# The place of a transpose, of a residual read and of an unpacking step in a fused linear-attention and FP4 MLP kernel

## Chip, core and metric

The kernel runs on one NeuronCore of a Trainium2 chip. Its time is the device time of one execution, in microseconds. Three executions of the kernel before took 1330.86 to 1332.29 us, with a median of 1332.18. In the text, TensorE is PE (its weight loads are PEld), VectorE is DVE, ScalarE is ACT, GpSimd is POOL and SyncE, which issues nearly all transfers, is SP.

## What is computed

The input x has 4 batches of 512 tokens of width 512, all float32. Two pre-norm layers follow each other:

```
x = x + attn(layernorm(x))        # gated linear attention, 4 heads of 128, chunks of 128 tokens
x = x + ffn(layernorm(x))         # GEGLU with FP4 weights, 512 -> 4096 -> 512

attn, per batch, head and chunk:
  q, k, v = x@Wq+bq, x@Wk+bk, x@Wv+bv;  k = k / |k|
  alpha = sigmoid(x@Walpha+balpha);  beta = softplus(x@Wbeta+bbeta)
  cla = cumsum(log(alpha))          # inside the chunk
  y   = (q k^T * beta * exp(cla - cla^T), causal) v  +  exp(cla) * (q state)
  state = state * exp(cla_end) + v^T (k * beta * exp(cla_end - cla))

ffn:  W = lut[4-bit code] * scale  (one scale per 32 values)
  inter = gelu(x Wg^T) * (x Wu^T);  out = inter Wd^T
```

## The kernel before

Attention comes first, with 16 chunks (4 batches of 4). The outer loop steps over batches b and, inside, over twelve products j: four of v, four of q, four of k, one for each 128 tokens or head. Behind each product stands a call behind(p) with a running step number p, which adds the attention work of one chunk in three steps:

- p % 3 == 0: chunk_lead transposes k to kT (PE, then a copy on ACT), chunk_values makes kw and vb on POOL, chunk_decay makes the decay matrix dm (four exponentials on ACT, a causal select on POOL), qc and the scaled state. Then turn("f") runs.
- p % 3 == 1: turn("a") for the first norm, then chunk_scores: the scores sp on PE and dm = sp * dm on DVE (L589).
- p % 3 == 2: chunk_sums: dp (the state's increment) and yp (the chunk's output) on PE, the residual sum (L616) and its write to HBM, the statistics of the second norm (L310, L312), the new state (L620 or L622); settle() then makes the normalised tile hn (L320, after two small POOL operations).

turn("f") takes the hn that the last chunk_sums left. It transposes it by four matmuls into one PSUM bank, tp_f (L341), splits the result into three float32r pieces g0, g1, g2 (ACT L362, DVE L363 and L364), and issues three writes of 256 KB to HBM, h (L366). hn keeps its buffer until then.

The MLP takes a float32 product as products of such pieces. It is cut into 35 rounds, i = 0 to 34. Round i works on batch i % 4 and on up to four MLP tiles of 128 columns. For each tile gate_up makes two products, gate and up: twelve 128x512 matmuls each into the banks pa and pb (L696), from twelve tiles x that hold the round's transposed tokens, read back from h. pb goes through ACT (L701) and the sum through DVE (L702) into t. Gate ends with a gelu (L706), up with the multiplication by gate (L711), the split into three inter tiles i (ACT L714, DVE L716 and L717), and a call unpack(slots, upto). After each of the two products gate_up yields, and behind(p) is called, so that the last batch's chunks run between the first MLP products. At the end of a round, down makes the second product in eight PSUM banks p_d (L731), two for each 128 tokens, adds them to the residual a4 (L744, L745) and writes it. Tiles of the round but the last are summed first. The residual is four reads of 256 KB from HBM, asked for when the round begins.

Rounds 0 and 1 have one and two tiles, because the window of tiles slides in; in round 30, which the code makes short, and in round 33 there are two as well. These are the rounds with fewer than three tiles. Round 0 has no down of its own.

unpack(slots, upto) first issues the rounding of a weight tile that is waiting (ACT L194), and then takes up to slots pieces from a queue that turns 4-bit codes into float32r weights (DVE L179, L184, L188, L197, L200), where a piece is due by the MLP tile number upto.

The order on every engine is the order of these calls. Two resources couple the engines. SBUF tiles of 2 KB and 4 KB per partition come from lists of 42 and 24 buffers, handed out in the order in which they were given back: whoever gets a buffer waits for its last reader, which can be a transfer. PSUM has eight banks, also handed out in the order in which they were freed.

Of the kernel before, what the change touches and what calls it, by code (L numbers as in the profile page):

```python
# [35 lines left out]
def f32(t):  # L36
    return t.bitcast(F32)
# [3 lines left out]
def tile_gated_linear_attention__then__nvfp4_geglu(  # L41
# [27 lines left out]
    MC = 4  # L69
# [13 lines left out]
    def pool(where, name, bufs, **kw):  # L83
        return where.enter_context(tc.tile_pool(name=name, bufs=bufs, reuse_waits="tile", **kw))
# [6 lines left out]
    slots = pool(ctx, "slots", 1)  # L91
# [31 lines left out]
    def psum(name):  # L123
        return fps.tile([P, T], F32, tag="p", name=name)
# [133 lines left out]
    def more():  # L258

        if not loaded or len(two_k.free) < 3:  # L260
            return
        nxt, start = loaded.pop(0)
        fields, masked, scaled, hi, lo, mi = start()

        def third():
            scaled()
            rounding.append(hi)

        def fourth():
            while rounding:  # L270
                rounding.pop(0)()
            lo()
            fetch()

        queue.insert(max(len(queue) - 2, 0), (0, fields))
        queue.extend([(0, masked), (nxt, third), (nxt, fourth), (nxt, mi)])

    def unpack(slots, upto):
        while rounding:
            rounding.pop(0)()  # L280
        for _ in range(slots):
# [17 lines left out]
    def tile_of(t):  # L299
        return xf[t * P : (t + 1) * P, :]  # L300
# [34 lines left out]
    def turn(which):  # L335
        for done in [t for t in turned if t[1][0] in which]:
            turned.remove(done)
            hn, key, use = done
            tp = psum(f"tp_{key}")
            for k in range(KC):  # L340
                nc.tensor.transpose(tp[:, k * P : (k + 1) * P], f32(hn)[:, k * P : (k + 1) * P], ident)  # L341
            one_k.put(hn)
            use(tp)
# [106 lines left out]
    def gates_exp(b):  # L450

        za, az, ea, u = (gate(b, nm) for nm in ("za", "az", "ea", "u"))
        zb = zs[b][:, :, H:]
        nc.vector.tensor_scalar(th(za), zs[b][:, :, :H], -80.0, None, ALU.max)
        nc.vector.scalar_tensor_tensor(th(az), zb, -1.0, zb, ALU.mult, ALU.max)
        return lambda: (
            nc.scalar.activation(ea, za, AF.Exp, scale=-1.0),
            nc.scalar.activation(u, az, AF.Exp, scale=-1.0),
        )
# [116 lines left out]
    def chunk_scores(b, n):  # L576
        toks = slice(n * P, (n + 1) * P)
        sp = psum(f"sp_{b}_{n}")
        kT = ch.pop("kT")
        for h in range(H):  # L580
            nc.tensor.matmul(  # L581
                sp[:, h * P : (h + 1) * P], f32(kT)[:, h * P : (h + 1) * P],
                f32(q_sb[b][h // 2])[:, h % 2, toks], start=True, stop=True,
            )
        one_k.put(kT)
        if n == NCH - 1:
            two_k.put(*q_sb[b])
        dm = ch["dm"]
        nc.vector.tensor_tensor(f32(dm), sp, f32(dm), ALU.mult)  # L589
# [42 lines left out]
    def behind(p):  # L632
        b, j = divmod(p, 3 * NCH)
        cb, n = divmod((p - 2 * NCH - 1) // 3, NCH)
        chunk = 0 <= cb < B
        first = b < B
        if p % 3 == 0:
            exps = gates_exp(b) if first and j == 3 else None
            if chunk:
                chunk_lead(cb, n)  # L640
                chunk_values(cb, n)
            if first and j == 6:
                exps = gates_sums(b)
            if chunk:
                chunk_decay(cb, n)
            turn("f")
            if exps:
                exps()
        elif p % 3 == 1:
            turn("a")  # L650
            if chunk:
                chunk_scores(cb, n)
            if first and j == 7:
                gates_end(b)
            for t in early.get(p + 4, ()):
                if t[0] > 1:
                    xs[t] = load(tile_of(t[0] * NCH + t[1]), f"x{t[0]}_{t[1]}")
            t = (p - 2 * NCH - 2) // 3 + 1
            if 0 <= t < NT:
                acc[divmod(t, NCH)] = load(tile_of(t), f"xr{t}")  # L660
        else:
            if first and j == 5:
                gates_ln(b)
            if chunk:
                chunk_sums(cb, n)
            for t in early.get(p, ()):
                first_norm(*t, xs.pop(t))
            settle()
# [11 lines left out]
    x3 = [[] for _ in rounds]  # L680

    def load_x(i, which):
        if i < len(rounds):
            for j, k in which:
                x3[i].append(load(h2d[i % B][j][k], f"x_{i}_{j}_{k}"))

    def gate_up(mt, x, slots, upto, last, key):
        w3 = wgu[mt]

        def product(i):  # L690
            pa, pb = psum(f"pa_{i}_{key}"), psum(f"pb_{i}_{key}")
            for o, js in ((pa, (0, 1)), (pb, (2,))):
                for j in js:
                    for k in range(KC):
                        c = 2 * i + k // 2
                        nc.tensor.matmul(  # L696
                            o, w3[j][:, k % 2, c * P : (c + 1) * P], x[j * KC + k],
                            start=(j == js[0] and k == 0), stop=(j == js[-1] and k == KC - 1),
                        )
            t = one_k.get(f"t{i}_{key}")  # L700
            nc.scalar.activation(f32(t), pb, AF.Copy, scale=-1.0 / ONE_E)  # L701
            nc.vector.tensor_tensor(f32(t), pa, f32(t), ALU.add)  # L702
            return t

        g = product(0)
        nc.scalar.activation(f32(g), f32(g), AF.Gelu_apprx_tanh, scale=ONE_E)  # L706
        unpack(slots, upto)
        yield
        u = product(1)
        last()  # L710
        nc.vector.scalar_tensor_tensor(f32(u), f32(g), ONE_E, f32(u), ALU.mult, ALU.mult)  # L711
        one_k.put(g)
        ih, il, im = (one_k.get(f"i{j}_{key}") for j in range(3))
        nc.scalar.activation(ih, f32(u), AF.Copy, scale=HI)  # L714
        unpack(slots, upto)
        nc.vector.tensor_tensor(il, f32(u), f32(ih), ALU.subtract)  # L716
        nc.vector.scalar_tensor_tensor(im, f32(ih), ONE_E, f32(u), ALU.mult, ALU.subtract)  # L717
        one_k.put(u)
        yield
        return ih, il, im  # L720

# [29 lines left out]
    def residual(i):  # L751
        return [
            load(accd[t], f"acc_{i}_{t}") for t in range(i % B * NCH, (i % B + 1) * NCH)
        ]

    def mlp():
        for i, r in enumerate(rounds):
            ts = range(i % B * NCH, (i % B + 1) * NCH)
            ms = tiles[i]
            inter = []  # L760
            a4 = residual(i) if i > 0 else None
            ahead = [0] if i >= B - 1 else [i] if i > 0 else []
            for q, mt in enumerate(ms):
                if q in ahead:
                    load_x(i + 1, jk[:6])

                def last():

                    if q == len(ms) - 1:
                        one_k.put(*x3[i])  # L770
                        load_x(i + 1, jk[len(x3[i + 1]) :] if i + 1 < len(rounds) else [])

                inter.append((yield from gate_up(mt, x3[i], 2 if i == 1 else 1, r + MC, last, f"{i}_{mt}")))
                if mt == r and mt < tiles[-1][0]:
                    two_k.put(*wgu[mt])
            final = i + B >= len(rounds)
            dst = [of[t * P : (t + 1) * P, :] if final else accd[t] for t in ts]
            if i == 0:
                over = ms, inter
                continue  # L780
            if i == B:
                ms, inter = over[0] + ms, over[1] + inter
            down(ms, inter, a4, dst, f"{i}", i == len(rounds) - 1)
            if r >= 0 and r % 2 == 1 and r < tiles[-1][0]:
                two_k.put(*wd[r // 2])
            yield
# [138 lines left out]
```

## Time and profile before

| | |
|---|---|
| runs (us) | 1332.29, 1332.18, 1330.86; median 1332.18 |
| profiled execution | 1330.86 us, its span 1329.1 us |
| granted TensorE clock, mean | 0.997 |
| chain that ended last | PE 89%, DVE 4%, POOL 2%, ACT 2%, issue 2%, DMA 1% |
| PE by line in that chain | pa L696 34%, p_d L731 25%, pb L696 17% |
| matmul L696, L731, 128x512 | 390 and 391 ns each, starts 0.227 us apart |
| DMA | 236.57 MB, mean 178 GB/s |

Busy time is the time in which an engine ran an instruction; matmuls overlap, so two of 390 ns can start 0.227 us apart. Attention with the start runs to about 240 us, the last batch's chunks lie between MLP products until about 305 us, and from then on the MLP rounds follow each other: each of them takes 32.6 us, with TensorE at work without a pause, as in the windows between 320 and 1200 us.

### The profile page before, as it was taken

To read this page: it belongs to the slowest core of one execution; us is meant where nothing else is said; L and a number is where in the kernel's file an instruction comes from. 1 tells how busy PE (TensorE), PEld (TensorE's weight loads), DVE (VectorE), ACT (ScalarE), POOL (GpSimd) and SP (SyncE) were. 2 spreads that over 40 slices of the span, in tenths; PEclk is the share of its full clock that TensorE was granted. 3 is DMA by queue.
4 is the path that set the end of the run, shared out by engine and by line. 5 is a ranking of instruction groups with operands and counts; after the bars stand their busy time and mean duration, and the time that the engine had idled before them with its cause. 6 is when DMAs were issued, how large, how long until landed. Compare 5 with 4: busy or idle time off the path is not lost.

```text
span 1329.1 us, 16898 instructions
## 1 busy us (share of the span) xinstructions
PE 1299.9 (98%) x5800; PEld 1041.1 (78%) x5800; DVE 974.8 (73%) x1533; ACT 441.8 (33%) x777; POOL 123.9 (9%) x220
## 2 busy tenths in 40 slices
PE   7999999889999999999999999999999999999998
PEld 5576666677888888888888888888888888887886
DVE  3477766677767777777777778787877777877556
ACT  1333323443333333333333333333333333332332
POOL 1446453520000000000000000000000000000000
PEclk9999999999999999999999999999999999999999
DMA  7034435667645565655565656465555555555463
GB/s 238 9 96 120 126 104 193 227 218 251 195 152 196 177 199 182 200 172 194 176 207 172 200 172 205 157 210 180 193 172 193 180 184 184 180 175 197 152 248 132
DMA packets 173798, 236.57 MB, mean 178 GB/s; under 512 B 15760, under 2 KB 74128, under 8 KB 173712
## 3 DMA queue, kind: packets, MB, share of 16 engines
q1 hardware_dynamic: 173008, 235.20, 54.2%
q8 instruction: 46, 0.75, 0.2%
q10 hardware_dynamic: 704, 0.28, 0.1%
q14 instruction: 40, 0.33, 0.1%
HBM read 183.00 MB, written 52.43 MB: 177 GB/s over the span
## 4 chain that ended last, share of the span: by engine, by line
PE 89%; DVE 4%; POOL 2%; ACT 2%; issue 2%; DMA 1%; POOLq 0%; ACTq 0%; DVEq 0%
PE pa L696 34%; PE p_d L731 25%; PE pb L696 17%; PE pq L406 4%; PE pva L381 2%; PE pvb L388 2%; PE pk L418 1%; PE sp L581 1%; PE tp_a L341 0%; ACT sq L426 0%; POOL ss L431 0%; PE yp L611 0%; PE yp L609 0%; PE tp_f L341 0%; DVE t L702 0%
## 5 line engine op out<-in xcount | busy, mean ns | idle before, releaser
L696 PE MATMUL pa<-x,wgu 128*128 128x512 f32 x2048 | 506.9, 390 | 0.1
L696 PEld LDWEIGHTS pa<-x,wgu 128*128 128x128 f32 x2048 | 383.7, 188 | 79.6 <-DVE acc L745 0.3
L731 PE MATMUL p_d<-wd,i 128*128 128x512 f32 x1536 | 358.4, 391 | 3.5 <-DVE i L716 2.5
L731 PEld LDWEIGHTS p_d<-wd,i 128*128 128x128 f32 x1536 | 289.5, 189 | 66.6 <-DVE i L716 3.5
L696 PE MATMUL pb<-x,wgu 128*128 128x512 f32 x1024 | 273.7, 389 | 0.0
L701 ACT ACTIVATE t<-pb 128x512 f32<-128x512 f32 x256 | 151.4, 591 | 355.1 <-PE pb L696 348.8
L702 DVE TENSOR_TENSOR t<-pa,t 128x512 f32<-128x512 f32 x256 | 176.6, 690 | 95.6 <-ACT t L701 90.2
L696 PEld LDWEIGHTS pb<-x,wgu 128*128 128x128 f32 x1024 | 192.2, 188 | 40.0
L744 DVE SCALAR_TENSOR_TENSOR acc<-p_d,acc 128x512 f32<-128x512 f32 x136 | 93.3, 686 | 111.0 <-PE p_d L731 111.0
L714 ACT ACTIVATE i<-t 128x512 fp32r<-128x512 f32 x128 | 81.0, 633 | 196.2 <-DVE t L711 194.7
L706 ACT ACTIVATE t<-t 128x512 f32<-128x512 f32 x128 | 81.1, 634 | 153.2 <-DVE t L702 153.2
L716 DVE TENSOR_TENSOR i<-t,i 128x512 fp32r<-128x512 f32 x128 | 88.2, 689 | 24.1 <-ACT i L714 22.5
L745 DVE TENSOR_TENSOR acc<-acc,p_d 128x512 f32<-128x512 f32 x136 | 93.6, 688 | 15.0 <-PE p_d L731 0.7
L711 DVE SCALAR_TENSOR_TENSOR t<-t,t 128x512 f32<-128x512 f32 x128 | 88.7, 693 | 4.4
L717 DVE SCALAR_TENSOR_TENSOR i<-i,t 128x512 fp32r<-128x512 f32 x128 | 87.7, 685 | 0.0
L418 PE MATMUL pk<-wk,hT 128*128 128x512 f32 x128 | 57.4, 592 | 0.0
L406 PE MATMUL pq<-hT,wq 128*128 128x512 f32 x128 | 57.2, 592 | 0.0
L406 PEld LDWEIGHTS pq<-hT,wq 128*128 128x128 f32 x128 | 23.3, 190 | 24.0 <-issue 23.9
L418 PEld LDWEIGHTS pk<-wk,hT 128*128 128x128 f32 x128 | 23.2, 190 | 23.5 <-issue 23.4
L197 DVE SCALAR_TENSOR_TENSOR wgu<-wgu,w_gu 128x1024 fp32r<-128x1024 f32 x32 | 38.9, 1217 | 1.7 <-ACT wgu L194 1.6
L188 DVE SCALAR_TENSOR_TENSOR w_gu<-i_gu,sc_gu 128x1024 f32<-128x1024 f16 x32 | 39.8, 1243 | 0.0
L200 DVE TENSOR_TENSOR wgu<-wgu,wgu 128x1024 fp32r<-128x1024 f32 x32 | 39.0, 1218 | 0.0
(121 smaller groups left out, 893.3 us busy)
## 6 DMA issues: line engine op xcount, KB each, us to landing
x<-h SPq DMA_DIRECT2D x420, 256.0 KB
acc<-acc SPq DMA_DIRECT2D x256, 256.0 KB
h<-g SPq DMA_DIRECT2D x48, 256.0 KB
x<-in_x SPq DMA_DIRECT2D x16, 256.0 KB
pk_gu<-in_gate_p SPq DMA_DIRECT2D x32, 128.0 KB
sc_gu<-in_gate_s SPq DMA_DIRECT2D x64, 64.0 KB
pk_gu<-in_up_p SPq DMA_DIRECT2D x32, 128.0 KB
sc_gu<-in_up_s SPq DMA_DIRECT2D x64, 64.0 KB
```

What stands on the lines that cost most here:

```text
L406: nc.tensor.matmul(pq, f32(wq[k // 2])[:, k % 2, h * P : (h + 1) * P], f32(hT[b][k // 2])[:, k % 2, :], start=(k == 0), stop=(k == KC - 1),)
L418: nc.tensor.matmul(pk, f32(hT[b][k // 2])[:, k % 2, n * P : (n + 1) * P], f32(wk[k // 2])[:, k % 2, :], start=(k == 0), stop=(k == KC - 1),)
L696: nc.tensor.matmul(o, w3[j][:, k % 2, c * P : (c + 1) * P], x[j * KC + k], start=(j == js[0] and k == 0), stop=(j == js[-1] and k == KC - 1),)
L701: nc.scalar.activation(f32(t), pb, AF.Copy, scale=-1.0 / ONE_E)
L702: nc.vector.tensor_tensor(f32(t), pa, f32(t), ALU.add)
L706: nc.scalar.activation(f32(g), f32(g), AF.Gelu_apprx_tanh, scale=ONE_E)
L711: nc.vector.scalar_tensor_tensor(f32(u), f32(g), ONE_E, f32(u), ALU.mult, ALU.mult)
L716: nc.vector.tensor_tensor(il, f32(u), f32(ih), ALU.subtract)
L717: nc.vector.scalar_tensor_tensor(im, f32(ih), ONE_E, f32(u), ALU.mult, ALU.subtract)
L731: nc.tensor.matmul(o, inter[i][j][:, n * P : (n + 1) * P], wd[ms[i] // 2][j][:, ms[i] % 2, :], start=(i == 0 and j == js[0]), stop=(i == L ...
L744: nc.vector.scalar_tensor_tensor(a, pas[2 * n], ONE_E, a, ALU.mult, ALU.add)
L745: nc.vector.tensor_tensor(a, a, pas[2 * n + 1], ALU.subtract)
```

## The change

Three instructions' places are changed, and no arithmetic.

First, turn("f") moves from the end of step p % 3 == 0 to step p % 3 == 1, behind the scores of the next chunk. Between the two places lies the next product. For all 16 chunks the four transposes, the three splits and the three writes follow later in the program, and hn keeps its buffer for longer.

Second, in round 1 (the second) the four reads of the residual are no longer issued when the round begins, but behind the round's last product, when the round's twelve x tiles have been given back, and ahead of the reads that remain of the next round's x. Other rounds are as before.

Third, for the last tile of a round with fewer than three tiles, unpack is called behind the three inter tiles instead of between the first and the second.

```
@@ behind(p)
             if chunk:
                 chunk_decay(cb, n)
-            turn("f")
             if exps:
                 exps()
         elif p % 3 == 1:
             turn("a")
             if chunk:
                 chunk_scores(cb, n)
+            turn("f")
@@ gate_up
-    def gate_up(mt, x, slots, upto, last, key):
+    def gate_up(mt, x, slots, upto, last, key, soon):
...
         nc.scalar.activation(ih, f32(u), AF.Copy, scale=HI)
-        unpack(slots, upto)
+        if not soon:
+            unpack(slots, upto)
         nc.vector.tensor_tensor(il, f32(u), f32(ih), ALU.subtract)
         nc.vector.scalar_tensor_tensor(im, f32(ih), ONE_E, f32(u), ALU.mult, ALU.subtract)
         one_k.put(u)
+        if soon:
+            unpack(slots, upto)
         yield
@@ mlp
-            a4 = residual(i) if i > 0 else None
+            a4 = residual(i) if i > 1 else None
...
                     if q == len(ms) - 1:
                         one_k.put(*x3[i])
+                        if i == 1:
+                            nonlocal a4
+                            a4 = residual(i)
                         load_x(i + 1, jk[len(x3[i + 1]) :] if i + 1 < len(rounds) else [])
 
-                inter.append((yield from gate_up(mt, x3[i], 2 if i == 1 else 1, r + MC, last, f"{i}_{mt}")))
+                inter.append((yield from gate_up(mt, x3[i], 2 if i == 1 else 1, r + MC, last, f"{i}_{mt}", mt == ms[-1] and len(ms) < 3)))
```

More of the change, by code (lines that the diff above doesn't have):

```diff
@@ L645, in behind @@
                 chunk_decay(cb, n)
-            turn("f")
             if exps:
@@ L652, in behind @@
                 chunk_scores(cb, n)
+            turn("f")
             if first and j == 7:
@@ L685, in load_x, with gate_up @@
                 x3[i].append(load(h2d[i % B][j][k], f"x_{i}_{j}_{k}"))
-    def gate_up(mt, x, slots, upto, last, key):
+    def gate_up(mt, x, slots, upto, last, key, soon):
         w3 = wgu[mt]
@@ L714, in gate_up @@
         nc.scalar.activation(ih, f32(u), AF.Copy, scale=HI)
-        unpack(slots, upto)
+        if not soon:
+            unpack(slots, upto)
         nc.vector.tensor_tensor(il, f32(u), f32(ih), ALU.subtract)
@@ L718, in gate_up @@
         one_k.put(u)
+        if soon:
+            unpack(slots, upto)
         yield
@@ L760, in mlp @@
             inter = []
-            a4 = residual(i) if i > 0 else None
+            a4 = residual(i) if i > 1 else None
             ahead = [0] if i >= B - 1 else [i] if i > 0 else []
@@ L770, in last @@
                         one_k.put(*x3[i])
+                        if i == 1:
+                            nonlocal a4
+                            a4 = residual(i)
                         load_x(i + 1, jk[len(x3[i + 1]) :] if i + 1 < len(rounds) else [])
-                inter.append((yield from gate_up(mt, x3[i], 2 if i == 1 else 1, r + MC, last, f"{i}_{mt}")))
+                inter.append((yield from gate_up(mt, x3[i], 2 if i == 1 else 1, r + MC, last, f"{i}_{mt}", mt == ms[-1] and len(ms) < 3)))
                 if mt == r and mt < tiles[-1][0]:
```

## The prediction

> **What bounds the kernel now.** I read the busy times first. TensorE is busy for 1299.9 of 1329.1 us, and the chain of work that ended last gives it 89%. Less arithmetic is not on offer, so the change can only win from TensorE's pauses.
>
> ```profile
> PE 1299.9 (98%) x5800; PEld 1041.1 (78%) x5800; DVE 974.8 (73%) x1533; ACT 441.8 (33%) x777; POOL 123.9 (9%) x220
> ```
>
> Then the waits of TensorE, longest in total first (us, times, longest):
>
> ```profile
> PE tp_f L341 <- DVE hn_f L320: 9.2, 6, 3.0
> PE yp L609 <- DVE dm L589: 4.3, 3, 3.5
> PE p_d L731 <- DVE i L716: 2.5, 2, 2.3
> PE p_d L731 <- DVE state L622: 0.4, 1, 0.4
> ```
>
> The rest (8 us) belongs to the start, which the change does not touch. The edits aim at the first three rows. TensorE's instructions in order of time say where these pauses lie (start, length, idle before it and its releaser):
>
> ```profile
> 266.47 0.63 PE L341 MATMUL tp_f<-ident,hn_f 128*128 128x128 f32 x4 [3.03 <-DVE hn_f L320]
> 277.85 0.46 PE L609 MATMUL yp<-vb,dm 128*128 128x128 f32 x2 [3.49 <-DVE dm L589]
> 284.42 3.26 PE L731 MATMUL p_d<-wd,i 128*128 128x512 f32 x13 [0.39 <-DVE state L622]
> 302.85 0.63 PE L341 MATMUL tp_f<-ident,hn_f 128*128 128x128 f32 x4 [2.16 <-DVE hn_f L320]
> 1220.33 4.63 PE L731 MATMUL p_d<-wd,i 128*128 128x512 f32 x11 [2.31 <-DVE i L716]
> ```
>
> Three smaller tp_f waits lie before 228 us (0.16, 0.61, 1.82), one at 248.91 (1.45), and two yp waits of 0.46 and 0.34 at 257.95 and 295.88. So the stretch to read is 228 to 320 us, where the last batch's chunks run between the first MLP products. There VectorE and ScalarE matter, because they run in program order:
>
> ```profile
> 241.45 0.69 DVE L589 TENSOR_TENSOR dm<-sp,dm 128x512 f32<-128x512 f32 x1 [1.28 <-POOL dm L540]
> 242.20 0.69 DVE L702 TENSOR_TENSOR t<-pa,t 128x512 f32<-128x512 f32 x1
> 266.96 0.81 DVE L711 SCALAR_TENSOR_TENSOR t<-t,t 128x512 f32<-128x512 f32 x1
> ```
> ```profile
> 267.85 0.63 ACT L714 ACTIVATE i<-t 128x512 fp32r<-128x512 f32 x1 [4.45 <-DVE t L711]
> 275.79 0.60 ACT L701 ACTIVATE t<-pb 128x512 f32<-128x512 f32 x1 [3.39 <-DMA h<-g]
> 1217.38 1.04 ACT L194 ACTIVATE wgu<-w_gu 128x1024 fp32r<-128x1024 f32 x1
> ```
>
> The 3.39 us on ScalarE is a buffer: t is given the place of a g piece whose transfer to HBM is still running. Last, the granted clock around the pauses (stretch, then busy times of PE, PEld, DVE, ACT, POOL, then clock, DMA share, GB/s):
>
> ```profile
> 264.00:266.00 2.00, 0.00 (x0) 0.00 (x0) 1.57 (x3) 0.00 (x0) 1.78 (x4) 1.00 0.54 185
> 280.00:282.00 2.00, 2.00 (x9) 1.71 (x8) 1.30 (x3) 0.63 (x1) 0.00 (x0) 0.50 0.97 345
> 1222.00:1223.00 1.00, 1.00 (x4) 0.81 (x3) 0.83 (x2) 0.00 (x0) 0.00 (x0) 0.50 0.03 8
> ```
>
> After the pauses of 3.49 and 2.31 us the matmuls ran for some 3 to 4 us at half clock; after 3.03 and 2.16 they did not.
>
> **The change part by part.** All times are on the clock of the profiled execution before (1330.86 us, of which 1329.1 is span; 1.3 below the median of 1332.18). The gain is how much earlier TensorE reaches the same instruction. A 128x512 matmul follows the last by 0.227 us (48 of them in 10.88).
>
> *1. The second norm's turn, up to 228 us.* Each of 16 turns moves four transposes (0.44 us on TensorE), one ScalarE copy (0.5), two VectorE splits (1.2) and three 256 KB writes behind the next product and its scores. Nothing is added. At the longest of the three waits the normalised tile came 1.82 us late, and in its new place it stands behind a product of 3.5 us and scores of 0.9, so the wait goes whole. What is late next would be the scores' kT (written at 187.5 to 188.1 while the scores would start at 191.1) and dm (GpSimd at 191.1, needed at 196.8): neither is. Gain 0.16+0.61+1.82 = 2.6.
>
> *2. The turn between 228 and 270 us.* Here the moved splits land badly. Before, g's two splits ran at 238.29 to 239.5, where VectorE then idled 1.28 us for GpSimd's dm at 241.45. In the new order they follow dm: 242.05 to 243.25, so t (L702), there at 242.20, starts at 243.25. Everything behind it on VectorE moves by 1.05 us: hn_f 248.22 to 249.25, k 248.68 to 249.7. ScalarE squares k (0.75 later) and then copies kT, done at 251.5, while TensorE, freed of the 1.45 wait, wants it at 250.65: a new wait of 0.9. GpSimd's kw, vb, dm and qc follow from that k and end at 257.65, 1.05 later; yp starts but pauses for dm and qc, about 0.9 in all, and ends at 259.3 instead of 259.76. VectorE regains part, as the splits no longer stand ahead of k at 255.17: dm 256.3, splits to 258.1, L188 to 259.2, t 259.2, L179, L197 at 261.55, then L616 at 262.7 (262.42 before). Its row of L616 to L711 takes 4.5 us as before, so L711 ends 0.3 later, ScalarE's L714 starts at 268.1 and kT ends at 269.2. TensorE has nothing else from 265.5: the scores wait 3.7 us where tp_f waited 3.03. The next product starts at 270.55 against 270.50. Gain of the three removed waits (1.45+0.46+3.03): 0. They are turned into waits on kT.
>
> *3. The residual of round two* (i = 1; round three is i = 2). Four 256 KB reads leave the queue at 256.35 and go behind the last product of the round. Four buffers stay free, and in the new handing-out t takes the place of xr13, whose write was issued at 263.12. The 3.39 us on ScalarE go: L701 runs at 272.1, after cd, t at 272.75, dm at 273.35 and done by 273.95, and yp starts at 274.2 instead of 277.85, with no half clock behind it. But the p_d block needs all eight banks, and its last two are freed by L616 and L622. VectorE: splits 275.2 to 276.4, L702 276.4, L711, L714, then i, i (277.9 to 279.8), L616 279.8 to 280.45, L622 to 282.0. TensorE stops at 278.0 until 280.45 and again to 282.0; the block ends at 282.0 + 13 x 0.227 = 284.95 against 284.42 + 13 x 0.227 = 287.4. Gain 2.4 (of 3.49 and some 1.8 of half clock). The reads themselves: behind g's writes (275.2 to 277.05), two wait for those to land (2.54 each in the chain), the last is issued at 279.1. At the 385 GB/s of the busiest stretch, landed by 282.5; L744 wants the first at 283.5. Covered by 1 us. The six reads of x behind them land at 286, wanted from 287.
>
> *4. Round three, 285 to 320 us.* L744 starts 2.4 earlier. tp_f stands behind the scores, its splits behind dm, so yp's 0.34 goes: yp at 292.5 (295.88). The last tp_f (2.16) moves behind one more product, and its tile is there at 299.8 just as TensorE is. The p_d block starts at 305.7 (311.52) and loses about 0.3 to the last i. Now the reads of x for round four bind: they follow the last g, written at 306.7, so they are issued at 307.4 as before (307.01) and need 10 us again (the transfers were dense from 306 to 317). Landed at 317.4, used by the last matmul of a group that takes 2.5: the round starts at 314.9 against 319.68. Gain since 228 us: 4.8, where the removed pauses and half clock sum to 13.
>
> *5. Unpacking behind inter.* It acts where a piece is due at a short round's last product. No piece stands there in round two or at 1296; at 1217 one does, L197, which waited 1.65 us for ScalarE's L194 and stood ahead of i. In the new order i follows L714 at once: 1217.5 and 1218.1, TensorE pauses 1.0 instead of 2.31 + 0.2, ten matmuls from 1218.8 end at 1221.05 instead of 1224.8, at full clock. L197 then delays L744 to 1219.9, and the bank it frees is wanted at 1221.05. x was landed by 1220.7. Gain 3.75.
>
> Sum 2.6 + 4.8 + 3.75 = 11.2: 1319.7 against the profiled 1330.86, so 1321.0 on the scale of the median.
>
> The clock speaks against the change in part 3: TensorE gets new pauses of 3.7 us at 265.5 and of 2.5 and 1.5 at 278 to 282. Half clock after the first is hidden (p_d waits for L616 anyway); after the second it costs up to 1.1, as in the row of 280 to 282. The Trainium skill, TensorE: Matmul & The Clock Gate, Part 1, says that the clock falls to half after an idle window of about 3.4 us, free-running. By that rule only the first new pause is long enough and the sum stays; by the rows, where 2.31 us sufficed, the sum is 10.1 and the time 1322.1. This trace agrees on the half and on the length, not on a threshold of 3.4.
>
> **The rivals.**
> - *VectorE is not that tight*, and the waits go without successors. For it: VectorE idles 1.28 and 3.22 us close by. All of it would be 9.2 + 3.5 + 1.8 + 0.8 + 0.4 + 3.75 = 19.5, so 1312.7. Against it: L702 at 242.20 follows dm immediately.
> - *The stretch from 228 to 320 gives nothing*: kT, L616 and the reads of x take the place of every pause, with half clock on top. Left are 2.6 + 3.75 = 6.35, so 1325.8. For it: part 2 comes to 0 already, and DMA is saturated around 306 to 317.
> - *Slower, by buffers*: hn is held one step longer, and a tile is given a place whose transfer still runs, as at 275.79. One such wait cost 3.39. To lose 0.2% (2.7) beyond the gain of 11.2 takes more than four of the 16 turns (13.9 / 3.39); at five the time is 1321.0 + 17.0 = 1338. Against it: in the changed program's handing-out the free buffers return in turn, and the t of that place gets an old one.
> - *No change within 0.2%* (1329.5 to 1334.9; 0.2% is about what a measurement can tell): the unpacking piece at 1217 still ends up ahead of i and the stretch gives nothing, so only 2.6 is left, 1329.6.
>
> **How the numbers follow.** Forecast 0.57 (its own range 1318.5 to 1323.5: one half clock, or a wait on kT 2 us shorter), rival one 0.12, rival two 0.20, slower 0.05, no change 0.06. Faster 0.89, same 0.06, slower 0.05. The range 1315.0 to 1327.5 takes in forecast and second rival with 1.7 to spare, and half of the way to the first.
>
> **What would show it.** Right: no tp_f wait of over 0.5 us outside the start; instead waits of sp on ScalarE's kT, about 0.9 and 3.7 us, and of p_d on L616 and L622, together about 3.6, near 278 to 282 (shifted by 2.6). No ScalarE wait on h<-g. The p_d wait near 1209 about 1 us at clock 1.00. Wrong: a yp wait of 3 us or more is left, the sp waits are missing (rival one), PE waits on reads of x or acc, or half clock near 1212.

## The result, and the profile after

The changed kernel took 1324.74 us (median of four; 1324.37 to 1324.83), against 1331.52 for the kernel before in the same comparison (1330.63 to 1332.29). The ratio is 0.9953, with a 95% interval of 0.9941 to 0.9966: 6.3 us less by the ratio and 6.8 by the two medians, where 11.2 were forecast. The time lies in the range of the prediction (1315.0 to 1327.5), but outside the forecast's own range (1318.5 to 1323.5), and nearer to the second rival (1325.8, the stretch from 228 to 320 us gives nothing) than to the forecast (1321.0). The profiled execution took 1324.66 us, of which its span is 1322.9.

From the changed kernel's page, the busy times; then its waits of TensorE (us in total, times, longest):

```profile
PE 1301.6 (98%) x5800; PEld 1040.2 (79%) x5800; DVE 975.4 (74%) x1533; ACT 441.8 (33%) x777; POOL 123.7 (9%) x220
```
```profile
PE sp L581 <- ACT kT L523: 5.2, 2, 3.5
...
PE p_d L734 <- DVE state L622: 0.8, 1, 0.8
PE pva L381 <- DVE v L396: 0.6, 2, 0.3
...
PE p_d L734 <- DVE i L717: 0.5, 2, 0.2
PE pb L696 <- DMA x<-h: 0.4, 2, 0.2
```

The waits on tp_f (9.2 us in all) and on yp (4.3) are gone. In their place stand waits of the scores on kT, as forecast, and small ones on v and on the first norm's tile (hn_a), on the state and on the reads of x. TensorE in order of time (start, length, idle before it and its releaser):

```profile
250.55 1.16 PE L581 MATMUL sp<-q,kT 128*128 128x128 f32 x8 [1.74 <-ACT kT L523]
253.88 2.40 PE L696 MATMUL pb<-x,wgu 128*128 128x512 f32 x4
268.66 2.07 PE L581 MATMUL sp<-q,kT 128*128 128x128 f32 x8 [3.51 <-ACT kT L523]
281.91 3.25 PE L734 MATMUL p_d<-wd,i 128*128 128x512 f32 x13 [0.78 <-DVE state L622]
316.77 0.50 PE L696 MATMUL pa<-x,wgu 128*128 128x512 f32 x1 [0.17 <-DMA x<-h]
1215.59 3.20 PE L734 MATMUL p_d<-wd,i 128*128 128x512 f32 x11 [0.23 <-DVE i L717]
```

The four matmuls at 253.88 take 2.40 us, where four of this kind take 1.07 at 260.65: the weight loads of the four (engine PEld) wait for a read of x each, 1.7 us in all.

The start differs from execution to execution (TensorE's first product of q begins at 27.31 us before and at 26.76 after), so I count gains from that product on. A gain at a place is how much less time TensorE took from its first product of q to there than in the profile before. An example: the end of the span is 1329.1 - 27.31 = 1301.79 us before and 1322.9 - 26.76 = 1296.14 after, so the gain over the span is 5.65. The same sum at seven places, for the change and for the runs told of below:

| gain of TensorE (us) at | forecast | change | turn alone | turn, t elsewhere | residual alone | turn and residual | turn ahead of scores |
|---|---|---|---|---|---|---|---|
| tpk of the last batch's first chunk (233.89 before) | 2.6 | 1.53 | 1.47 | 1.49 | 0.04 | 1.47 | 3.21 |
| tpk of its third chunk (262.60) | 3.1 | 0.49 | 1.30 | 1.22 | 0.04 | 0.09 | 3.70 |
| the product behind the third chunk's scores (270.50) | 2.6 | -1.29 | -1.09 | -1.29 | -1.55 | -1.52 | 3.36 |
| tpk of its last chunk (287.52) | 5.0 | 1.97 | -4.66 | 0.86 | 2.41 | 1.54 | 5.83 |
| p_d of round three (311.52) | 8.4 | 4.74 | -1.81 | 3.70 | 1.03 | 4.38 | 7.16 |
| p_d of round four (341.44) | 7.4 | 2.11 | -4.14 | 1.50 | 1.03 | 1.61 | 5.16 |
| end of the span | 11.15 | 5.65 | -5.45 | 1.17 | 1.27 | 1.64 | 8.66 |

Between round four and 1200 us the gains stay the same to 0.01 in every run, so all of the change happens before 341 us and at 1217. Single profiles of the same program differ by up to 1.2 us in the stretch from 250 to 305 (four that have the changed kernel's program up to there, the change's own and three of the section on the reads of x, gained 0.23 to 1.42 us at 262.60 and 1.96 to 2.79 at 287.52), and the kernel before by more (the unpacking alone has the old program up to 1200 us and stood 1.54 lower at 341).

Now the engines behind. VectorE and then ScalarE after:

```profile
239.36 0.69 DVE L589 TENSOR_TENSOR dm<-sp,dm 128x512 f32<-128x512 f32 x1 [2.47 <-POOL dm L540]
239.97 0.68 DVE L363 TENSOR_TENSOR g<-tp_f,g 128x512 fp32r<-128x512 f32 x1
244.13 0.69 DVE L717 TENSOR_TENSOR i<-t,i 128x512 fp32r<-128x512 f32 x1 [1.56 <-DMA h<-g]
248.21 0.55 DVE L320 TENSOR_SCALAR hn_f<-xr,mv_f,rs_f 128x512 f32<-128x512 f32 x1 [0.44 <-POOL rs_f L315]
299.60 0.55 DVE L320 TENSOR_SCALAR hn_f<-xr,mv_f,rs_f 128x512 f32<-128x512 f32 x1 [0.99 <-POOL rs_f L315]
305.60 0.68 DVE L363 TENSOR_TENSOR g<-tp_f,g 128x512 fp32r<-128x512 f32 x1
```
```profile
271.41 0.62 ACT L701 ACTIVATE t<-pb 128x512 f32<-128x512 f32 x1
...
275.71 0.60 ACT L701 ACTIVATE t<-pb 128x512 f32<-128x512 f32 x1 [1.24 <-PE pb L696]
...
303.92 0.58 ACT L362 ACTIVATE g<-tp_f 128x512 fp32r<-128x512 f32 x1
```

The wait of 3.39 us of L701 on a write of g is gone from ScalarE, but one of 1.56 of the same kind has come up on VectorE at 244.13. It was in no step of the prediction. Round one's inter tiles take the buffers that held g of the third batch's last chunk, and those writes now start later. hn_f, behind it, is finished at 248.8 us as before, although dm, ahead of it on VectorE, starts two microseconds earlier (239.36 against 241.45). And the last chunk's hn is ready 2.6 us earlier than before (299.60 against 302.16), while its first copy on ScalarE starts at 303.92. The same copy in the kernel before:

```profile
303.88 0.58 ACT L362 ACTIVATE g<-tp_f 128x512 fp32r<-128x512 f32 x1
```

It started at 303.88 there. Counted from the first product of q, hn is 2.0 us earlier than before and this copy 0.6 us later. The granted clock after (stretch, busy times of the five engines; the last three numbers are clock, DMA share and GB/s):

```profile
268.00:270.00 2.00, 1.34 (x6) 1.34 (x7) 2.00 (x4) 1.97 (x4) 0.00 (x0) 0.50 0.90 337
270.00:272.00 2.00, 2.00 (x10) 1.90 (x10) 0.35 (x1) 2.00 (x6) 0.86 (x2) 0.50 0.09 33
272.00:274.00 2.00, 2.00 (x7) 1.52 (x6) 1.29 (x2) 1.97 (x4) 2.00 (x3) 0.50 0.00 0
...
1217.00:1219.00 2.00, 2.00 (x10) 1.64 (x9) 1.90 (x4) 0.00 (x0) 0.00 (x0) 1.00 0.69 255
```

After the pause of 3.51 us TensorE ran at half clock until 274, and after the pause at 1215 at full clock.

### The profile page after: what moved, and what is told of

It reads as the page before. It is cut to its first block, busy times and chain, and to the rows that moved or that the text cites. A ratio compares the mean times of both kernels' runs of the same rounds, so it can differ in the third digit from the quotient of the medians.

```text
span 1322.9 us, 16906 instructions
## 1 busy us (share of the span) xinstructions
PE 1301.6 (98%) x5800; PEld 1040.2 (79%) x5800; DVE 975.4 (74%) x1533; ACT 441.8 (33%) x777; POOL 123.7 (9%) x220
## 4 chain that ended last, share of the span: by engine, by line
PE 93%; DVE 3%; DMA 2%; POOL 1%; issue 1%; ACT 1%; SPq 0%; DVEq 0%; ACTq 0%; POOLq 0%
PE pa L696 34%; PE p_d L734 25%; PE pb L696 17%; PE pq L406 4%; PE pk L418 3%; PE pva L381 2%; PE pvb L388 2%; DMA x<-h 1%; PE sp L581 1%; PE yp L609 1%; PE yp L611 1%; PE dp L600 1%; PE tp_a L341 1%; PE tp_f L341 0%; PE tpk L520 0%
## 5 line engine op out<-in xcount | busy, mean ns | idle before, releaser
L701 ACT ACTIVATE t<-pb 128x512 f32<-128x512 f32 x256 | 151.3, 591 | 349.2 <-PE pb L696 346.5
L702 DVE TENSOR_TENSOR t<-pa,t 128x512 f32<-128x512 f32 x256 | 176.6, 690 | 95.4 <-ACT t L701 90.1
L714 ACT ACTIVATE i<-t 128x512 fp32r<-128x512 f32 x128 | 81.0, 633 | 198.2 <-DVE t L711 195.1
L717 DVE TENSOR_TENSOR i<-t,i 128x512 fp32r<-128x512 f32 x128 | 88.2, 689 | 25.9 <-ACT i L714 22.7
L711 DVE SCALAR_TENSOR_TENSOR t<-t,t 128x512 f32<-128x512 f32 x128 | 88.7, 693 | 4.4
```

## The experiments: each part alone

Theory: each of the three parts gives what the prediction gave it. Rivals: a part alone gives all, or the parts need each other.

**The turn alone** (the changed kernel without the second part, and with soon False everywhere):

```
-            a4 = residual(i) if i > 1 else None
+            a4 = residual(i) if i > 0 else None
...
-                        if i == 1:
-                            nonlocal a4
-                            a4 = residual(i)
```

> Only the second norm's turn is moved. Theory (the stretch from 228 to 320 us goes by VectorE's and ScalarE's order and by buffers): TensorE reaches 228 us 2.1 us earlier, as in the changed kernel, and loses that again on kT and on a buffer still being written to HBM; the wait of yp near 278 stays. 1329.5 to 1332, no gain that can be told. Rival (the waits that were removed are simply gone): the 9.2 us of tp_f waits come off, 1322 to 1324.

Measured: 1334.43 us, ratio 1.0028 (1.0018 to 1.0038). It is slower than the kernel before, by 3.7 us, and both expectations fell. ScalarE, and then TensorE with its clock, in this run:

```profile
280.17 0.60 ACT L701 ACTIVATE t<-pb 128x512 f32<-128x512 f32 x1 [3.75 <-DMA h<-g]
```
```profile
284.85 1.00 PE L734 MATMUL p_d<-wd,i 128*128 128x512 f32 x2 [2.81 <-DVE xr L616]
286.37 5.83 PE L734 MATMUL p_d<-wd,i 128*128 128x512 f32 x13 [0.52 <-DVE state L622]
```
```profile
288.00:290.00 2.00, 2.00 (x7) 1.52 (x6) 1.85 (x4) 0.00 (x0) 0.00 (x0) 0.50 0.01 3
```

Round two's last t waits for a buffer whose g is still being written, 3.75 us, since that write starts later. L616 stands behind it, p_d's last banks are late by 2.81 us, and the thirteen matmuls behind that pause take 5.83 us at half clock instead of 3.26. What was the prediction's third rival (slower by buffers) happens here, at one buffer.

**The residual alone** (the changed kernel with turn("f") in its old place, and with soon False everywhere):

```
             if chunk:
                 chunk_decay(cb, n)
+            turn("f")
...
                 chunk_scores(cb, n)
-            turn("f")
```

> Only the residual of round two is moved. Theory: the 3.39 us wait of ScalarE on h<-g goes and VectorE is some 2.4 us earlier in round two; the tp_f waits stay. A gain of 2 to 3, 1328.5 to 1329.5. Rival (the reads are late for L744): a wait of VectorE on acc, no gain or a loss, 1331 or more. Rival (the whole yp wait with its half clock comes off): 5 us, 1326.5.

Measured: 1329.37 us, ratio 0.9990 (0.9981 to 0.9999), 1.4 us less than before. In the table it gains the 2.4 of the prediction's part 3 at 287.5 and gives 1.4 of it back in the next round, where ScalarE's L701 waits 2.25 us at 291.22 for a buffer that a transfer of the residual sum still uses (acc<-acc).

**The unpacking alone** (turn and residual as before, the call of unpack as changed):

> Only unpack is moved behind inter in short rounds. Theory: the wait of p_d on i in round 30 falls from 2.31 to about 0.2 with no half clock behind it, 3.5 us as in the changed kernel, 1328.0. Rival (the time comes back in the next round, where the weights are ready later): under 1 us, 1331.

Measured: 1328.20 us, ratio 0.9983 (0.9974 to 0.9992), 2.5 us less. In the profiles the step is worth 3.5: 2.02 + 1.54 = 3.56 there, and 5.65 - 2.11 = 3.54 in the whole change, against 3.75 forecast.

The three parts alone sum to +3.7 - 1.4 - 2.5 = -0.2 us, and together they give -6 to -7. So something between them is worth 6 us.

## The experiments: what the turn and the residual have to do with each other

**Turn and residual without the unpacking** (the changed kernel with soon False everywhere):

> The changed kernel with the unpacking where it was (turn and residual moved, nothing else). The single parts summed to -0.2 us and the whole change is worth -6.0 to -6.8. Theory (turn and residual need each other: moved alone, the turn hands t a buffer whose g is still being written, and the residual's move gives back four buffers and takes that wait away): without the unpacking the gain is the whole less the 2.5 that the unpacking gave alone, 1327 to 1328.5. Rival (the interaction is with the unpacking, or shared): 1330 or more if turn and residual just add up (+3.7 - 1.4 = 1333).

Measured: 1328.39 us against 1331.24 before, ratio 0.9980 (0.9972 to 0.9989): 2.9 us less, where the parts alone would give +2.3. The interaction is between these two.

**The turn alone, with another buffer for one tile**. Only the t of round two's last product is moved, to the list of 4 KB buffers:

```
         def get(self, name):
-            if not self.free:
+            if not self.free or (self.spare and name == "t1_1_1"):
```

> The kernel with the turn alone moved (residual and unpacking as before), but round two's last t takes its buffer from the list of 4 KB buffers, where no transfer is running. Theory (the turn alone lost 3.7 us because t waited for a g that was still being written, 3.75 us at 280.2): that wait is gone, the two pauses of TensorE behind it (2.81 on L616 and the half clock from 286 to 292) shrink to under 1 us, the last chunk's transposes of k come 3 to 4 us earlier (292.0), and the time is 1329.0 to 1331.5. Rival (the loss is in the kT waits or in the transfers that the later writes of g disturb): 1333 to 1335, as with the turn alone.

Measured: 1329.72 us, ratio 0.9993 (0.9984 to 1.0002). One buffer for one tile is worth 0.35% (1.0028 to 0.9993), 4.7 us. ScalarE in this run:

```profile
275.56 0.58 ACT L362 ACTIVATE g<-tp_f 128x512 fp32r<-128x512 f32 x1
276.04 0.59 ACT L701 ACTIVATE t<-pb 128x512 f32<-128x512 f32 x1
```

L701 follows L362 at once. Behind it p_d's pauses are 1.27 and 0.78 us (the expectation had the first under 1), with no half clock. With that wait out of the way the parts add up, as far as intervals of 1.2 us to each side can tell: the turn 1.5 and the residual 1.4 make 2.9, the measured 2.9. So the second part of the change does two things: it removes a wait that the kernel before had, and it gives back the four buffers without which the first part is a loss.

**Other buffers for round one's inter tiles**, in the changed kernel, against the new wait of 1.56 us (skip is 3 for the three i tiles of round one, else 0):

```
-            tag = self.free.pop(0)
+            tag = self.free.pop(skip)
```

> The changed kernel, but round one's three inter tiles take the buffers behind the three that g of chunk 12 has just left. Theory (that buffer wait of 1.56 us is what swallowed the first 2.1 us): VectorE has no wait on h<-g near 244, hn_f and kT come 0.8 to 1.2 earlier, and TensorE is as much earlier up to the reads of x for round four, which follow the last g and so come earlier too. 1323.5 to 1324. Rival (GpSimd or the reads of x of round two are as late anyway): 1324.7, the time of the changed kernel.

Measured: 1324.73 us, ratio 0.9952 (0.9939 to 0.9964), the time of the changed kernel. The wait is gone (L717 waits 0.70 us for ScalarE's i instead). VectorE's hn_f and TensorE's scores of the third chunk in this run:

```profile
246.74 0.55 DVE L320 TENSOR_SCALAR hn_f<-xr,mv_f,rs_f 128x512 f32<-128x512 f32 x1 [0.44 <-POOL rs_f L315]
```
```profile
267.19 2.07 PE L581 MATMUL sp<-q,kT 128*128 128x128 f32 x8 [3.67 <-ACT kT L523]
```

Counted from the first product of q, both come 0.9 to 1.3 us earlier than in the seven profiles in which the turn stands behind the scores and the wait is there, as the theory had it. TensorE then waits for x in six places, 1.3 us in all, and still keeps more in this profile (3.36 at round four, where the change has 2.11). But the profiled execution is the fastest of its five (1323.31 to 1326.39 us), and their median is that of the change. So the wait holds up VectorE and the scores by about 1 us; that the time is shorter without it is not shown.

**Which of VectorE's work stands where.** In the changed kernel VectorE waits 2.47 us for GpSimd at 239.36 and only then makes g's splits. Here the turn goes ahead of the scores instead:

```
             turn("a")
+            turn("f")
             if chunk:
                 chunk_scores(cb, n)
-            turn("f")
```

> The changed kernel, with turn("f") between turn("a") and the chunk's scores instead of behind the scores. VectorE then makes g's two splits ahead of dm, in the 2.47 us that it idled for GpSimd's dm at 239.4 in the changed kernel. Theory (part 2 of the prediction lost its gain to the splits behind dm): TensorE is 1 to 2 us earlier at the transposes of k of the last chunk (285.0), the scores' waits on kT fall below 3 us in sum (5.2), and of this 0.5 to 1.5 us reach the end, because round three's last g is also written earlier: 1323.2 to 1324.2. Rival (those waits come from VectorE's whole row of work, wherever the splits stand): the waits on kT or on hn_f stay at 5 us or more, 1324.5 to 1326.

Measured: 1321.42 us, ratio 0.9932 (0.9920 to 0.9945), better than the theory's range. VectorE and then TensorE:

```profile
238.28 0.68 DVE L364 SCALAR_TENSOR_TENSOR g<-g,tp_f 128x512 fp32r<-128x512 f32 x1
238.88 0.68 DVE L589 TENSOR_TENSOR dm<-sp,dm 128x512 f32<-128x512 f32 x1
...
242.25 0.69 DVE L717 TENSOR_TENSOR i<-t,i 128x512 fp32r<-128x512 f32 x1 [1.36 <-DMA h<-g]
```
```profile
265.56 2.08 PE L581 MATMUL sp<-q,kT 128*128 128x128 f32 x8 [1.92 <-ACT kT L523]
273.44 0.46 PE L609 MATMUL yp<-vb,dm 128*128 128x128 f32 x2 [1.61 <-DVE dm L589]
```

The splits lie in the idle time ahead of dm. Of the two waits on kT (5.2 us) one is left, of 1.92, and yp waits of 1.61 and 1.02 are back. From 40 to 228 us the trace shows no wait of TensorE, where the changed kernel has three, of 0.32, 0.27 and 0.34: the gain there is 3.2 instead of 1.5. That is more than the three waits removed (2.6): the gain comes in three steps of 0.36, 0.80 and 2.0 us where tp_f waited 0.16, 0.61 and 1.82, so each removed wait gives 0.2 us more than the idle time listed for it.

**Both**, the turn ahead of the scores and the other buffers:

> The kernel with turn("f") ahead of the scores, and round one's inter tiles in buffers that no transfer is reading (they wait 1.36 us for a write of g at 242.25 there). Theory (that wait is on the path, since hn and k stand behind it on VectorE): VectorE reaches hn 1.0 to 1.4 us earlier (246.1), the wait of the scores on kT at 265.6 (1.92) or the one on dm at 273.4 (1.61) shrinks, and 0.4 to 1.2 us reach the end: 1320.2 to 1321.0. Rival (as behind the scores, where it gave nothing, since a later wait takes its place): 1321.1 to 1321.8.

Measured: 1321.71 us, ratio 0.9931 (0.9917 to 0.9945). Again the wait of 1.36 goes, and again the time does not move. TensorE in this run:

```profile
264.16 1.16 PE L581 MATMUL sp<-q,kT 128*128 128x128 f32 x8 [1.92 <-ACT kT L523]
272.04 0.46 PE L609 MATMUL yp<-vb,dm 128*128 128x128 f32 x2 [3.09 <-DVE dm L589]
```

The wait on kT has the same length, and the next one on dm is 1.5 longer. TensorE came to it sooner, in part because it ran at full clock here behind the wait on kT (the eight scores take 1.16 us, and 2.08 in the other run). In this profile the stretch is bound by VectorE and ScalarE in program order, and what TensorE reaches earlier it waits for later.

## The experiments: the reads of x for round four

In the changed kernel TensorE is 4.7 us ahead at round three's p_d, but only 2.1 at round four's. The reads of round four's x bind there. Two explanations: they share the transfer engines with what else is moved at 314 to 319 us (theory), or they come at their own rate behind the last g, and that is late (rival).

**Round three's writes later**, behind round four's first up product:

```
+            if key == "2":
+                held.append((dst[n], a4[n]))
+            else:
+                nc.sync.dma_start(dst[n], a)
...
+                    if i == 3 and q == 0:
+                        write_held()
```

> The changed kernel with the four writes of round three's sums (256 KB each) issued behind round four's first up product instead of as each sum is ready; they then no longer share the transfer engines with round four's reads of x. Theory (those writes delay the reads): the last x lands 1 to 2 us earlier (319.3 in the changed kernel), round four's first pb ends by 318.5 to 319 instead of 320, and the time is 1322.7 to 1323.9. Rival (the reads come as fast as they are issued, behind the last g, and the writes cost them nothing): TensorE reaches round four's second product at the same time within 0.4 us, 1324.3 to 1325.1.

Measured: 1325.35 us, ratio 0.9958 (0.9944 to 0.9971): no change. It did not test the theory, because the next reads took the place of the writes at once, so I held those back too.

**The residual reads and the next x behind that product as well**:

```
-            a4 = residual(i) if i > 1 else None
-            ahead = [0] if i >= B - 1 else [i] if i > 0 else []
+            a4 = residual(i) if i > 1 and i != 3 else None
+            ahead = [1] if i == 3 else [0] if i >= B - 1 else [i] if i > 0 else []
...
                     if i == 3 and q == 0:
+                        a4 = residual(i)
                         write_held()
```

> The changed kernel, in which nothing else is transferred beside round four's twelve reads of x: the four writes of round three's sums, round four's four residual reads and the six early reads of round five's x all go behind round four's first up product. (With the writes alone moved, the residual reads and the next x took their place on the transfer engines at once, so that run did not test it.) Theory (the reads of x are late because they share the transfer engines): the twelve alone are 3.1 MB, 8.2 us at 385 GB/s; they land 1.5 to 2.5 us earlier than 319.3, round four's first pb has no wait, its second product starts at 317.5 to 318.3 instead of 319.7, and the time is 1322.3 to 1323.4. Rival (they are late because the last g is, and come at their own rate whatever runs beside them): the second product moves by less than 0.5 us, 1324.2 to 1325.2.

Measured: 1324.31 us, ratio 0.9953 (0.9940 to 0.9965), again no change; in the profile the second product starts 0.4 us earlier than in the changed kernel. This was no clean test either: to be behind a product in the program delays nothing on SyncE, which had nothing to wait for and issued the residual reads at 314.15 and the writes at 316.86.

**All of it at round four's last product**, and behind buffers that are still in use:

```
+            ahead = [] if i == 3 else [0] if i >= B - 1 else [i] if i > 0 else []
...
                         load_x(i + 1, jk[len(x3[i + 1]) :] if i + 1 < len(rounds) else [])
+                        if i == 3:
+                            a4 = residual(i)
+                            write_held()
```

> The changed kernel, in which round four's reads of x are alone by what stands behind them on SyncE, too: all twelve reads of round five's x, then round four's residual, then the four held writes are asked for at round four's last product, behind the packed weights of the round (0.5 MB). (In the two runs before, what was moved behind a product was still issued at 314 to 317 us, since SyncE had nothing to wait for there, so 1 to 2 MB still ran beside the reads.) With TensorE's first product of q taken as the zero of all the runs, round four's second product starts at 319.7 in the changed kernel (first q 26.76) and 319.2 in the run before (26.70). Theory (they share the transfer engines): 317.3 to 318.5, no wait of pb on x over 0.1 us, and 1322.3 to 1323.5 if the later reads bind nothing. Rival (the reads come at their own rate behind the last g): 318.9 to 319.7, and 1323.9 to 1325.

Measured: 1325.53 us, ratio 0.9957 (0.9944 to 0.9970). Now the reads are nearly alone: by the profile's GB/s some 0.5 MB of other transfers run with their 3.15 MB. SyncE's queue, TensorE, and the window behind the reads:

```profile
308.69 6.33 SPq L296 DMA_DIRECT2D x<-h  x12
315.71 0.38 SPq L213 DMA_DIRECT2D pk_gu<-in_gate_p  x1
323.46 1.26 SPq L218 DMA_DIRECT2D sc_gu<-in_gate_s  x2
```
```profile
320.44 0.50 PE L696 MATMUL pb<-x,wgu 128*128 128x512 f32 x1 [0.16 <-DMA x<-h]
320.78 1.99 PE L696 MATMUL pa<-x,wgu 128*128 128x512 f32 x8
```
```profile
320.00:322.00 2.00, 1.84 (x8) 1.32 (x8) 0.39 (x1) 0.60 (x1) 0.00 (x0) 1.00 0.03 10
```

From 320 us the transfer engines are all but idle (10 GB/s), and the matmul that waits for the last x starts at 320.44. The second product starts 320.78 - 27.89 = 292.89 us behind the first product of q; in the changed kernel it is 319.71 - 26.76 = 292.95. The theory is refuted: the twelve reads need some 11.7 us from their first issue (308.69 to 320.4) without the writes and the residual reads, too. From 309 to 319 us the transfer engines show busy shares of 0.89 to 1.06, so these reads fill them almost by themselves. When they begin is set by the last g, behind whose writes they stand in SyncE's queue, and that is held by the order on ScalarE and VectorE: L362 at 303.92 stands behind L701 and L714 of one more product, and L363 at 305.60 (304.49 before) behind that product's L702, L711, two inter tiles and an unpacking step.

**The turn ahead of the scores, the other buffers, and the writes and reads of the second of these runs**:

> All of it: turn("f") ahead of the scores, other buffers for round one's inter tiles, and round four's reads of x alone on the transfer engines. Theory (with the reads no longer late, what is gained before 305 us reaches the end): by the 2.1 us that round four's first product loses with the turn ahead of the scores, 1319.0 to 1320.2. Rival (the reads come at their own rate): 1320.8 to 1321.8.

Measured: 1320.83 us, ratio 0.9925 (0.9913 to 0.9938). It is the fastest version, faster than both kernels; by the intervals it can't be told from the turn ahead of the scores alone (0.9920 to 0.9945). Not tried: to leave only the last chunk's turn in its old place, which would make its g earlier at the price of a tp_f wait.

## Why the prediction was right, and where it was not

The direction, the list of removed waits and their successors on kT and on the state were right. The size was not: the forecast gained 11.15 and the profile 5.65. That the time lies in the range is owed to the range's width, which was drawn to take in the second rival, and not to the sum. Of the signs of being wrong that the prediction named, one came: TensorE waits on reads of x (0.6 us in all). By the forecast's own steps:

| step | forecast | measured | what it rests on |
|---|---|---|---|
| 1, turn up to 228 us | 2.6 | 1.53 | 1.46 to 1.55 in the eight profiles with this order |
| 2, turn from 228 to 270 us | 0 | -2.8 | 1.53 to -1.29 (at 270.50) |
| 3, residual of round two | 2.4 | 3.3 | -1.29 to 1.97 |
| 2 and 3 together | 2.4 | 0.4 | 1.53 to 1.97; 0.4 to 1.3 in the four profiles of this program |
| 4, round three and the reads of x | 2.4 | 0.14 | 1.97 to 2.11 |
| 5, unpacking | 3.75 | 3.54 | 2.11 to 5.65 |

*Step 1* asked only whether kT and dm are late next. What is late next is the first norm's tile, and v, whose L396 on VectorE stands behind an unpacking step (2.04 us at 189.85) while the bank that it frees is wanted at 192.28. Three such waits (0.93 us in all) stand where tp_f waited:

```profile
128.98 0.63 PE L341 MATMUL tp_a<-ident,hn_a 128*128 128x128 f32 x4 [0.32 <-DVE hn_a L320]
131.21 2.05 PE L381 MATMUL pva<-wva,hT 128*128 128x264 f32 x8 [0.27 <-DVE v L396]
192.28 2.05 PE L381 MATMUL pva<-wva,hT 128*128 128x264 f32 x8 [0.34 <-DVE v L396]
```

*Step 2* had the splits behind dm, and the waits on kT that follow, in the right places: 1.74 and 3.51 us measured, 0.9 and 3.7 forecast. The failed step is that it took the buffers of the inter tiles as free. VectorE waits 1.56 us for a write of g at 244.13, and hn_f behind it starts 0.5 us later than before, counted from the first product of q, where the forecast had it 1.6 earlier (2.6 - 1.05). Of these 2.1 us, 1.1 are missing since step 1, and about 1 is this wait: with other buffers hn_f and the third chunk's scores come 0.9 to 1.3 us earlier. Two more losses lie in this stretch. The reads of x for round two are issued from 243.56 (240.63 before), behind the later writes of g, and cost 1.3 us at 253.88. And half clock behind the pause of 3.51 makes the way from the scores to the next product 2.58 us long, against 1.35 at the chunk before. The prediction followed the handing-out only for the t in which the profile of before showed a wait. The run with the turn alone shows how much can hang on one such place: 4.7 us.

*Step 3*. The 3.39 us on ScalarE went and the yp wait too, as forecast; p_d paused 0.78 us, less than the 3.6 forecast in all. What failed is "half clock after the first is hidden", at least in part. TensorE ran at half clock from 268.66 to 274, ScalarE's L701 waited 1.24 us for that product at 275.71, and L616, which p_d needs, stands behind it. Of the four profiles of this program, that of the run with the reads nearly alone had its clock back sooner (0.88 from 272 to 274 us). L701 does not wait for that product there, and the gain at 287.52 is 2.79, against 1.96 to 2.00 in the other three. So the clock cost some 0.8 us of the 2.0 that the two steps lack. With the residual alone both steps together gave 2.4, although TensorE was 1.55 behind at 270.50: there the half clock was hidden.

*Step 4* had the right mechanism (the reads of x bind, they follow the last g) and the wrong time. The forecast put g's end at 306.7 and the issue at 307.4 on a time scale from which step 1's 2.6 was still to be taken; the trace shows 306.9 and 307.36 with everything included. The row of L362 says why: hn's earlier end does not reach g, since the turn now stands behind one more product. And the reads took 11.7 us even when they were nearly alone, where the prediction read 10 off the kernel before; why they are longer is open.

*Step 5* was right: the pause fell from 2.31 to 0.23, better than the 1.0 forecast, and the half clock behind it went.

The second rival described the stretch well: it gave 2.11 - 1.53 = 0.6 us. Its sum with step 1 as measured would be 1.53 + 3.54 = 5.1, close to the 5.65. The first rival (waits go without successors) is out. The third (slower by buffers) does not hold for the change but does for its first part alone.

On the clock, the prediction weighed the rule of the Trainium skill, TensorE: Matmul & The Clock Gate, Part 1 (half clock after an idle window of some 3.4 us that runs freely) against the row of 2.31 us. The runs fit a window whose place is not tied to the pause: the same wait before the same matmuls gave half clock before, and full clock with turn and residual. TensorE and the clock there:

```profile
1218.96 3.17 PE L734 MATMUL p_d<-wd,i 128*128 128x512 f32 x11 [2.31 <-DVE i L717]
```
```profile
1220.00:1222.00 2.00, 2.00 (x11) 1.63 (x10) 1.79 (x4) 0.00 (x0) 0.00 (x0) 1.00 0.09 36
```

3.17 us instead of 4.63 for the same eleven matmuls. So the 1.5 us of half clock in step 5's gain are not there in every execution, which may be why the unpacking alone measured 2.5 and not 3.5; that was not shown. That half clock follows 2.31 us in four profiles shows that a pause need not reach 3.4 us for it.

## What to carry to other kernels

When buffers are handed out in the order of release, a store that starts later makes a wait at whoever gets its buffer next, so a moved store is followed to all takers of its buffers, and two edits that look independent can need each other through the free list. A step moved behind a wait of its engine loses what it gains; it belongs into the idle time ahead of that wait (here 2.47 us ahead of dm; the run with the turn there took some 3 us less than the change, about half of it before 228 us, where other waits went). An earlier input does not bring an output forward when the copies between them stand behind other work in program order, and a transfer that is written later in the program is not issued later if its queue has nothing to wait for.

## What was not expected of the hardware

The granted clock fell to half after pauses of 2.3 us in some executions and not in others. The same holds for waits of 1.92 us on kT (half clock with the turn ahead of the scores, full clock when round one's inter tiles had other buffers, too) and for the wait on tp_f near 266 us. That was 3.03 us in the kernel before, and the eight matmuls of pa behind it took 2.09 us; with the residual alone it was 3.04, and they took 3.64 us at a clock of 0.50:

```profile
265.50 0.76 PE L341 MATMUL tp_f<-ident,hn_f 128*128 128x128 f32 x4 [3.04 <-DVE hn_f L320]
```

Behind all eight pauses of 3.36 to 4.27 us between 260 and 280 us, each in another profile, the clock was at half. The wait on the last tp_f is one more such pair: 2.16 us in the kernel before, with the clock at 1.00 behind it, and 2.18 with the unpacking alone, with half clock (TensorE, then the clock):

```profile
302.30 0.63 PE L341 MATMUL tp_f<-ident,hn_f 128*128 128x128 f32 x4 [2.18 <-DVE hn_f L320]
```
```profile
304.00:306.00 2.00, 2.00 (x7) 1.52 (x6) 1.22 (x2) 0.00 (x0) 0.00 (x0) 0.50 0.47 134
```

Twelve reads of 256 KB took about 11.7 us from the first issue to the last landing with some 0.5 MB of other transfers beside them, some 270 GB/s (3.15 MB / 11.7 us), although the engines moved up to 409 GB/s in single microseconds of that stretch.
